# A graph-attention and a multi-head layer on one core: the order of the seven products in the projections, and when two helpers' additions may run

## The chip, the core and the metric

The kernel runs on one core of a Trainium2 chip. The metric is device time in microseconds. Before the change the median of three runs is 2658.33 us (2658.18 to 2658.8). All arithmetic is in float32. A core has a matrix engine (TensorE, in the profile PE for its products and PEld for its weight loads), a vector engine (VectorE, DVE), a scalar engine (ScalarE, ACT), GpSimd (POOL) and queues of transfers. [...]

## The reference

Input x is (64, 256, 512): 64 graphs of 256 nodes with 512 features. One adjacency matrix (256, 256) serves all. Two residual layers follow each other:

```python
# layer 0
h = jnp.maximum(_layernorm(x, axis=-1), 0.0)
x = x + _L0_gnn_ref(h, adj, L0_gnn_W, L0_gnn_a)        # one graph attention head, output [alpha@hW, hW]
# layer 1
h = jnp.maximum(_layernorm(x, axis=-1), 0.0)
x = x + _L1_gnn_ref(h, adj, Wq, bq, Wk, bk, Wv, bv, Wo, bo)

# inside layer 1, for 8 heads of 64
q = split_heads(h @ Wq.T + bq); k = split_heads(h @ Wk.T + bk); v = split_heads(h @ Wv.T + bv)
scores = jnp.einsum('bhqd,bhkd->bhqk', q, k) / 8
attn = softmax(where(adj == 0, -inf, scores))
return (attn @ v).reshape(b, n, 512) @ Wo.T + bo
```

## The kernel before

Two graphs make a group; there are 32 groups. The projections q, k and v of a group, and the output projection, are each a product of two matrices cut into quadrants, done with seven products of quadrants in place of eight (Winograd's form of Strassen's algorithm). For that, sums of the operand's quadrants are needed, made once per group by GpSimd for q, k and v, and by VectorE for the output:

```python
def not_sooner(engine, operation, *args, **kwargs):
    last = engine.last                       # the engine's last instruction so far
    after(getattr(engine, operation)(*args, **kwargs), last)

def operand_sums(engine, quads, sums):
    a11, a12, a21, a22 = quads
    not_sooner(engine, "tensor_add", sums[:, 0], a21, a22)
    engine.tensor_sub(sums[:, 1], sums[:, 0], a11)
    engine.tensor_sub(sums[:, 2], a11, a21)
    engine.tensor_sub(sums[:, 3], a12, sums[:, 1])

def seven(quads, sums):
    a11, a12, _, a22 = quads
    s1, s2, s3, s4 = (sums[:, i] for i in range(4))
    return {
        1: (a11, W11), 2: (a12, W21), 3: (s4, W22), 4: (a22, T4),
        5: (s1, T1), 6: (s2, T2), 7: (s3, T3),
    }
```

The program's scheduler is free to run an instruction of an engine ahead of one that was written earlier, if its data are there. `not_sooner` forbids that: the instruction comes after the one that was last on this engine when it was written. TensorE's whole order is fixed as written.

A projection adds the seven products up in two accumulators (PSUM banks), with copies of intermediate states kept by ScalarE and additions by VectorE:

```python
first = blocks(held_bank(turn[0], f"p{name}1_{g}"))
product(first, 1, True)
p1 = kept(first, 0, 0)                       # ScalarE: bank -> SBUF, with the bias
yield
second = blocks(mm(f"p{name}2_{g}"))
product(second, 2, True)
vector.tensor_add(part(0, 0), second, p1)
yield
product(first, 6, False)                     # onto product 1
p16 = kept(first, 0, 1)
yield
second = blocks(held_bank(1 - turn[0], f"p{name}7_{g}"))
product(second, 7, True)
p7 = kept(second, 1, 2)
yield
product(first, 5, False)
vector.tensor_add(part(1, 1), first, p7)
yield
product(second, 4, False)
vector.tensor_add(part(1, 0), second, p16)
yield
product(first, 3, False)
take(part(0, 1), first, 1)                   # ScalarE
yield
```

Each `yield` ends a piece. Pieces of different groups are interleaved by strings, one for each of the four steps of a group:

```python
steps = ("Suuunuonuonuuo", "Sssnuosuosouso", "Sususuososuos", "sSsuuousouounuonsu")
for g in range(NG):
    products = project(g + 1) ...            # "u": pieces of q, then k, then v of the next group
    pieces = first_layer(g + 2) ...          # "s": layer 0 of the group after next
    for step, parts in enumerate(steps):
        ...weigh(*waiting)                   # attention of the step before: totals, reciprocal, oT
        for part in parts: ...               # "S": scores, "o": a piece of the output projection,
                                             # "n": a piece of the next norm
        if step == 0 and g + 1 < NG:
            residual(g + 1)                  # x + b_out
```

In the first step the three "n" are: two rows' statistics, their rstd (a power on GpSimd) and normed rows xn; then their transposes xt on VectorE; then a ReLU copy hT on ScalarE. `scores` ends with two additions ps on GpSimd, after VectorE's multiplication by the mask. `residual` adds the output bias to four tiles of rows:

```python
def residual(g):
    for b in range(GB):
        for t in range(NT):
            xt = xs[g, b][:, t, :]
            gpsimd.tensor_add(xt, xt, b_out)
```

Of the kernel before, what the change touches and what calls it, by code (L numbers as in the profile page):

```python
# [57 lines left out]
def bounded(  # L58
# [24 lines left out]
    vector, scalar, gpsimd = (Remembers(e) for e in (nc.vector, nc.scalar, nc.gpsimd))  # L83
# [23 lines left out]
    def mm(name):  # L107
        return psum.tile([P, 512], F32, tag="turn", name=name, bufs=5)

    def held_bank(n, name):  # L110
        return psum.tile([P, 512], F32, tag=f"held{n}", name=name, bufs=1)

    def after(instruction, name):

        tc.add_manual_dep(
            instruction.ins, name,
            mybir.DependencyInfo(mybir.DependencyClass.NoSync, mybir.DependencyReason.DATA),
            reason="the engine's order",
        )

    def not_sooner(engine, operation, *args, **kwargs):

        last = engine.last
        after(getattr(engine, operation)(*args, **kwargs), last)
# [9 lines left out]
    def matmul(*args, **kwargs):  # L134
        in_order(nc.tensor.matmul(*args, **kwargs))  # L135
# [80 lines left out]
    b_out = const.tile([P, D], F32, name="b_out")  # L216
# [203 lines left out]

    def operand_sums(engine, quads, sums):
        a11, a12, a21, a22 = quads
        not_sooner(engine, "tensor_add", sums[:, 0], a21, a22)
        engine.tensor_sub(sums[:, 1], sums[:, 0], a11)
        engine.tensor_sub(sums[:, 2], a11, a21)
        engine.tensor_sub(sums[:, 3], a12, sums[:, 1])

    def seven(quads, sums):
# [32 lines left out]
    def first_layer(g):  # L461
# [36 lines left out]
        for r in range(GT):  # L498
# [28 lines left out]
            hT[:, 2 * c : 2 * c + 2, r * N : (r + 1) * N] for r in range(2) for c in range(2)  # L527
        ]
        operand_sums(gpsimd, quads, sums)
        operands[g] = seven(quads, sums)  # L530
        yield

    def residual(g):

        for b in range(GB):
            for t in range(NT):
                xt = xs[g, b][:, t, :]
                gpsimd.tensor_add(xt, xt, b_out)


    places = [f"place{i}" for i in range(8)]
# [1 line left out]
    def place(shape, name):  # L543
        tag = places.pop(0)
        return big.tile(shape, F32, tag=tag, name=name, bufs=1), tag
# [4 lines left out]
    def project(g):  # L550
        ops = operands.pop(g)
        for name in ("q", "k", "v"):
            shape = [P, NT, D] if name == "v" else [P, HP, N]
            dst = {}
            for b in range(GB):
                dst[b], tag = place(shape, f"{name}_{g}_{b}")
                qkv[name, g, b] = dst[b], tag
            turn[0] = 1 - turn[0]

            def blocks(bank):  # L560
                return bank.rearrange("p (o n) -> p o n", o=2)

            def product(out, i, start):
                a, w = ops[i][0], w_sb[name][:, :, ops[i][1], :]
                for o in range(2):
                    cols = slice(o * P, (o + 1) * P)
                    for c in range(2):
                        of, by = (a[:, c, cols], w[:, c, :]) if name == "v" else (w[:, c, cols], a[:, c, :])
                        matmul(
                            out[:, o, :], of, by, start=start and o == c == 0, stop=o == c == 1,  # L570
                            skip_group_check=True,
                        )

            def part(b, half):
                if name == "v":
                    return dst[b][:, :, half * D // 2 : (half + 1) * D // 2]
                return dst[b][:, 2 * half : 2 * half + 2, :]

            def take(to, bank, half):
                if name == "v":  # L580
                    scalar.copy(to, bank)
                    return
                for o in range(2):
                    i = 2 * half + o
                    scalar.activation(
                        to[:, o, :], bank[:, o, :], AF.Identity,
                        bias=bcol[name][:, i : i + 1], scale=1.0,
                    )

            def kept(bank, half, i):  # L590
                s = att.tile([P, 2, N], F32, tag="kept", name=f"kept{i}_{name}_{g}")
                take(s, bank, half)
                return s

            first = blocks(held_bank(turn[0], f"p{name}1_{g}"))
            product(first, 1, True)
            p1 = kept(first, 0, 0)
            yield
            second = blocks(mm(f"p{name}2_{g}"))
            product(second, 2, True)  # L600
            vector.tensor_add(part(0, 0), second, p1)
            yield
            product(first, 6, False)
            p16 = kept(first, 0, 1)
            yield
            second = blocks(held_bank(1 - turn[0], f"p{name}7_{g}"))
            product(second, 7, True)
            p7 = kept(second, 1, 2)
            yield
            product(first, 5, False)  # L610
            vector.tensor_add(part(1, 1), first, p7)
            yield
            product(second, 4, False)
            vector.tensor_add(part(1, 0), second, p16)
            yield
            product(first, 3, False)
            take(part(0, 1), first, 1)
            yield
# [29 lines left out]
    def weigh(g, b, quad, p, ps):  # L648


        v, v_tag = qkv["v", g, b]
        name = f"{g}_{b}_{quad}"
        total = mm(f"total_{name}")[:, :N]
        for j in range(QH):
            matmul(
                total[j * S : (j + 1) * S, :], ones[:, :S], ps[:, j, :], start=True, stop=True
            )
        r = att.tile([P, N], F32, tag="r", name=f"r_{name}", bufs=1)
        vector.reciprocal(r, total)
        pr = mm(f"pr_{name}").rearrange("p (h n) -> p h n", h=2)  # L660
        for half in range(2):
            for kb in range(NT):
                for j in range(QH):
                    c0 = (quad * QH + j) * DH + half * S
                    matmul(
                        pr[j * S : (j + 1) * S, half, :], v[:, kb, c0 : c0 + S], p[:, j, kb, :],
                        start=(kb == 0), stop=(kb == NT - 1),
                    )
        oT = big.tile([P, 2, N], F32, tag=f"oT{quad}", name=f"oT_{name}", bufs=1)
        vector.tensor_mul(oT, pr, r[:, None, :].to_broadcast([P, 2, N]))  # L670
        oTs[quad] = oT
        if quad == NQ - 1:
            places.append(v_tag)
            quads = [oTs[c][:, :, r * P : (r + 1) * P] for r in range(2) for c in range(2)]
            sums = big.tile([P, 4, 2, P], F32, tag="o_sums", name=f"o_sums_{g}_{b}", bufs=1)
            operand_sums(vector, quads, sums)
            operands["o", g, b] = seven(quads, sums)
# [51 lines left out]
    for piece, _ in enumerate(first_layer(0)):  # L729
# [7 lines left out]
        elif piece == 11:  # L737
            weight_sums("q")
    residual(0)
    products, pieces = project(0), first_layer(1) if NG > 1 else iter(())  # L740
    for i, part in enumerate("nssnsssssssssssnsn---"):
        next(products)
# [5 lines left out]
    run(verdict)  # L748


    steps = ("Suuunuonuonuuo", "Sssnuosuosouso", "Sususuososuos", "sSsuuousouounuonsu")
    waiting, late = None, iter(())
    for g in range(NG):
        products = project(g + 1) if g + 1 < NG else iter(())
        pieces = first_layer(g + 2) if g + 2 < NG else iter(())
        for step, parts in enumerate(steps):
            b, quad = divmod(step, NQ)
            if waiting is not None:
                weigh(*waiting)
                if waiting[2] == NQ - 1:  # L760
                    late = outputs(*waiting[:2])
            for part in parts:
                if part == "u":
                    next(products, None)
                elif part == "o":
                    next(late, None)
                elif part == "s":
                    next(pieces, None)
                elif part == "n":
                    next(norms, None)  # L770
                else:
                    waiting = (g, b, quad, *scores(g, b, quad))
            if step == 0 and g + 1 < NG:
                residual(g + 1)
            if step % 2 == 0 and g + 3 < NG:
                load(g + 3, b)
        run(products)
        run(pieces)
# [373 lines left out]
```

## Time and profile before

The profiled execution has a span of 2657.8 us.

| engine | busy us | share of the span |
|---|---|---|
| TensorE products (PE) | 2546.2 | 96% |
| TensorE weight loads (PEld) | 2035.1 | 77% |
| VectorE (DVE) | 1892.7 | 71% |
| GpSimd (POOL) | 993.7 | 37% |
| ScalarE (ACT) | 829.5 | 31% |

In the lines of the profile that follow, a line in the order of time begins with the start and the duration in us, then the engine, the line of the source (nearly all have the line of a helper, so the names tell them apart), the operation, output<-inputs by the program's names, the shape and the number of instructions merged in the line; in brackets the idle time of the engine before it, and what ended it. A line in the table of waits has the engine and what it was about to write, whom it waited for, and then the sum of the waits in us, their number and the longest.

The groups are alike in the middle of the run. In the stretch from 1090.5 to 1171.0 us, one group, PE was busy 78.51 of 80.50 us, DVE 58.79, POOL 30.94 and ACT 25.68.

### The profile page before, as it was taken

How to read it: one execution, taken by the hardware profiler on the slowest of the kernel's cores; microseconds unless marked ns; L12 is line 12 of the kernel's file. 1: busy time of each engine (PE TensorE's matmuls, PEld its weight loads, DVE VectorE, ACT ScalarE, POOL GpSimd, SP SyncE). 2: the span in 40 equal slices, each digit the busy share in tenths (PEclk: the TensorE clock that was granted, in tenths of full speed). 3: DMA queues.
4: the chain of work that ended last, by engine and by line, in shares of the span. 5: the costliest groups of instructions: out<-in, count | busy, mean ns of one | idle time of the engine just before them, and what ended most of it. 6: DMA issues, size and time to landing. Idle time of an engine off the chain costs nothing.

```text
span 2657.8 us, 41200 instructions
## 1 busy us (share of the span) xinstructions
PE 2546.2 (96%) x16158; PEld 2035.1 (77%) x16158; DVE 1892.7 (71%) x3103; ACT 829.5 (31%) x1759; POOL 993.7 (37%) x816
## 2 busy tenths in 40 slices
PE   6899999999999999999999999999999999999998
PEld 4677777777777777777777777877777777777776
DVE  5667678767677776687776787676777766777756
ACT  1333323333323333333233233333233333332321
POOL 3333343333343343444333434333433433433422
PEclk9999999999999999999999999999999999999999
DMA  5111222212222212222212222112222122222110
GB/s 178 48 48 64 96 80 93 83 56 72 93 83 83 82 59 80 81 95 80 72 64 88 80 96 80 64 64 96 80 88 87 57 73 88 88 80 80 47 35 33
DMA packets 129350, 205.37 MB, mean 77 GB/s; under 512 B 13952, under 2 KB 78208, under 8 KB 129152
## 3 DMA queue, kind: packets, MB, share of 16 engines
q1 hardware_dynamic: 129152, 202.69, 22.7%
q8 instruction: 129, 2.11, 0.3%
q14 instruction: 69, 0.57, 0.1%
HBM read 104.08 MB, written 98.57 MB: 76 GB/s over the span
## 4 chain that ended last, share of the span: by engine, by line
PE 53%; DVE 28%; POOL 9%; issue 7%; ACT 2%; DMA 1%; SPq 0%; DVEq 0%; ACTq 0%; POOLq 0%
PE pq L135 11%; PE py L135 10%; PE ph L135 8%; PE pv L135 7%; PE pk L135 7%; POOL sums L35 6%; PE pr L135 4%; DVE r L35 4%; PE sc L135 4%; DVE x L35 4%; DVE xn L35 3%; DVE xt L35 3%; DVE p L35 3%; POOL rstd L35 3%; DVE st L35 2%
## 5 line engine op out<-in xcount | busy, mean ns | idle before, releaser
L35 POOL TENSOR_TENSOR ps<-p 128x512 f32<-128x512 f32 x256 | 361.3, 1421 | 770.8 <-DVE p L35 770.8
L35 DVE TENSOR_TENSOR p<-p,maskT 128x1024 f32<-128x1024 f32 x256 | 434.1, 1717 | 48.3 <-ACT p L35 48.1
L35 DVE TENSOR_TENSOR x<-py,x 128x256 f32<-128x256 f32 x448 | 185.5, 414 | 350.9 <-PE py L135 343.9
L35 ACT ACTIVATE p<-sc 128x512 f32<-128x512 f32 x512 | 267.1, 602 | 382.3 <-PE sc L135 382.3
L135 PE MATMUL pq<-sums,wq_sb 128*128 128x256 f32 x1024 | 244.5, 388 | 59.2 <-POOL sums L35 59.2
L35 POOL TENSOR_TENSOR rstd<-ve,rexp 128x2 f32<-128x2 f32 x128 | 120.7, 943 | 449.9 <-DVE ve L35 444.5
L135 PE MATMUL sc<-q,k 64*128 64x256 f32 x2048 | 286.5, 393 | 0.0
L135 PEld LDWEIGHTS pq<-sums,wq_sb 128*128 128x128 f32 x1024 | 194.9, 193 | 97.6 <-POOL sums L35 71.6
L135 PEld LDWEIGHTS sc<-q,k 64*128 64x128 f32 x2048 | 203.9, 186 | 83.8 <-issue 52.6
L135 PE MATMUL py<-wo_sb,o_sums 128*128 128x256 f32 x1024 | 262.8, 380 | 2.5 <-DVE x L35 2.5
L35 DVE TENSOR_SCALAR xn<-x,mv,rstd 128x512 f32<-128x512 f32 x256 | 179.0, 730 | 109.1 <-POOL rstd L35 107.9
L135 PE MATMUL pr<-p,v 128*32 128x256 f32 x4096 | 245.5, 379 | 0.0
L135 PE MATMUL ph<-w_sb,hT 128*128 128x258 f32 x1024 | 243.6, 385 | 1.0 <-ACT hT L35 1.0
L135 PE MATMUL pv<-wv_sb,sums 128*128 128x256 f32 x1024 | 241.7, 379 | 0.0
L135 PE MATMUL pk<-sums,wk_sb 128*128 128x256 f32 x1024 | 240.2, 382 | 0.0
L35 DVE RECIPROCAL r<-total 128x256 f32<-128x256 f32 x128 | 223.3, 1744 | 16.1 <-PE total L135 16.1
L135 PEld LDWEIGHTS ph<-w_sb,hT 128*128 128x128 f32 x1024 | 192.9, 191 | 38.7 <-ACT p L35 9.9
L135 PEld LDWEIGHTS pk<-sums,wk_sb 128*128 128x128 f32 x1024 | 191.8, 190 | 35.2 <-issue 10.3
L35 POOL TENSOR_TENSOR x<-x,b_out 128x512 f32<-128x512 f32 x128 | 198.2, 1558 | 53.1 <-DVE xn L35 31.8
L135 PEld LDWEIGHTS pv<-wv_sb,sums 128*128 128x128 f32 x1024 | 194.5, 190 | 26.6 <-DVE v L35 0.3
L135 PEld LDWEIGHTS py<-wo_sb,o_sums 128*128 128x128 f32 x1024 | 192.0, 190 | 29.0 <-DVE x L35 3.3
L135 PE MATMUL py<-wo_sb,oT 128*128 128x256 f32 x768 | 200.2, 384 | 12.0 <-DVE x L35 12.0
(118 smaller groups left out, 3583.8 us busy)
## 6 DMA issues: line engine op xcount, KB each, us to landing
passed<-xt SPq DMA_DIRECT2D x124, 512.0 KB, 2.7
moved<-passed SPq DMA_DIRECT2D x496, 128.0 KB, 2.9
x<-in_x_dram SPq DMA_DIRECT2D x64, 512.0 KB, 3.9
out_dram<-x SPq DMA_DIRECT2D x64, 512.0 KB, 2.8
wq_sb<-in_L_gnn_Wq_dram SPq DMA_DIRECT2D x2, 512.0 KB, 11.9
wk_sb<-in_L_gnn_Wk_dram SPq DMA_DIRECT2D x2, 512.0 KB, 12.1
wv_sb<-in_L_gnn_Wv_dram SPq DMA_DIRECT2D x2, 512.0 KB, 11.6
wo_sb<-in_L_gnn_Wo_dram SPq DMA_DIRECT2D x8, 128.0 KB, 2.8
```

Source lines behind the costliest of these rows:

```text
L35: instruction = getattr(self.engine, operation)(*args, **kwargs)
L135: in_order(nc.tensor.matmul(*args, **kwargs))
```

## The change

The products of each projection come in the order 1, 2, 7, 6, 4, 5, 3. Product 7 needs only the difference a11 - a21, so that difference is made first, and the helper says so with `not_sooner`. The purpose is that TensorE has a product to do while GpSimd makes the sums that product 6 needs. The string of the first step is rearranged to suit. The additions of b_out, which the scheduler could run as soon as their rows were free, are held behind what GpSimd was last given to do.

```diff
     def operand_sums(engine, quads, sums):
         a11, a12, a21, a22 = quads
+        not_sooner(engine, "tensor_sub", sums[:, 2], a11, a21)
         not_sooner(engine, "tensor_add", sums[:, 0], a21, a22)
         engine.tensor_sub(sums[:, 1], sums[:, 0], a11)
-        engine.tensor_sub(sums[:, 2], a11, a21)
         engine.tensor_sub(sums[:, 3], a12, sums[:, 1])
@@ residual
-                gpsimd.tensor_add(xt, xt, b_out)
+                not_sooner(gpsimd, "tensor_add", xt, xt, b_out)
@@ project
-            product(first, 6, False)
-            p16 = kept(first, 0, 1)
-            yield
             second = blocks(held_bank(1 - turn[0], f"p{name}7_{g}"))
             product(second, 7, True)
-            p7 = kept(second, 1, 2)
+            p7 = kept(second, 1, 1)
+            yield
+            product(first, 6, False)
+            p16 = kept(first, 0, 2)
+            yield
+            product(second, 4, False)
+            vector.tensor_add(part(1, 0), second, p16)
             yield
             product(first, 5, False)
             vector.tensor_add(part(1, 1), first, p7)
-            yield
-            product(second, 4, False)
-            vector.tensor_add(part(1, 0), second, p16)
             yield
             product(first, 3, False)
             take(part(0, 1), first, 1)
@@ steps
-    steps = ("Suuunuonuonuuo", "Sssnuosuosouso", "Sususuososuos", "sSsuuousouounuonsu")
+    steps = ("Suuununuonuouo", "Sssnuosuosouso", "Sususuososuos", "sSsuuousouounuonsu")
```

## The prediction

> **What bounds the kernel now.** I read the page's shares first, then the table of waits, then the order of time on TensorE (PE), GpSimd (POOL) and VectorE (DVE) around one group's start.
>
> ```profile
> PE 2546.2 (96%) x16158; PEld 2035.1 (77%) x16158; DVE 1892.7 (71%) x3103; ACT 829.5 (31%) x1759; POOL 993.7 (37%) x816
> ```
>
> TensorE is the bound: 96% busy, one fixed instruction order, granted clock 0.994. The table of waits says what interrupts it:
>
> ```profile
> PE pq L135 <- POOL sums L35: 59.2, 31, 7.5
> PE py L135 <- DVE x L35: 14.5, 34, 1.2
> ```
>
> 31 waits of the query projection for GpSimd's sums, one at each group but the first. In order of time, around 1090 us, TensorE alone:
>
> ```profile
> 1090.62 3.72 PE L135 MATMUL pq<-hT,wq_sb 128*128 128x256 f32 x16
> 1096.02 3.72 PE L135 MATMUL pq<-sums,wq_sb 128*128 128x256 f32 x16 [1.68 <-POOL sums L35]
> ```
>
> Sixteen matmul records are products 1 and 2, so a product is 8 records; a single one started at 1100.44 and the next work at 1102.17, so a product holds TensorE 1.73 us. TensorE could have gone on at 1090.62 + 2 x 1.73 = 1094.08 and goes on at 1096.02: 1.94 us lost per group. The same three numbers return 80.5 us later, again and again: the steady period is 80.5 us. Now GpSimd and VectorE in the same stretch:
>
> ```profile
> 1090.95 2.82 POOL L35 TENSOR_TENSOR sums<-hT 128x512 f32<-128x512 f32 x2 [5.33 <-ACT hT L35]
> 1093.72 2.24 POOL L35 TENSOR_TENSOR sums<-sums,hT 128x512 f32<-128x512 f32 x1
> 1096.04 2.13 POOL L35 TENSOR_TENSOR sums<-hT,sums 128x512 f32<-128x512 f32 x1
> 1098.14 2.50 POOL L35 TENSOR_TENSOR ps<-p 128x512 f32<-128x512 f32 x2
> 1100.59 0.71 POOL L35 TENSOR_TENSOR rstd<-ve,rexp 128x2 f32<-128x2 f32 x1
> ```
> ```profile
> 1092.56 4.49 DVE L35 TENSOR_TENSOR p<-p,maskT 128x1024 f32<-128x1024 f32 x2
> ...
> 1101.34 1.00 DVE L35 TENSOR_SCALAR xn<-x,mv,rstd 128x512 f32<-128x512 f32 x2 [1.87 <-POOL rstd L35]
> 1102.26 0.41 DVE L35 TENSOR_TENSOR x<-py,x 128x256 f32<-128x256 f32 x1
> 1102.59 1.29 DVE L35 STREAM_TRANSPOSE xt<-xn 128x512 f32<-128x512 f32 x2
> 1103.81 0.65 DVE L35 TENSOR_TENSOR q<-pq,kept_q 128x512 f32<-128x512 f32 x1
> 1104.38 0.41 DVE L35 TENSOR_TENSOR x<-py,x 128x256 f32<-128x256 f32 x1
> ```
>
> GpSimd's order is sums 0 and 2 (both read hT alone), then 1, then 3. Product 6 needs sum 1, the third, which ends at 1095.96. Product 7 needs only sum 2. Second thing to see: the engines' small DVE chain xn, xt hangs on GpSimd's rstd at 1101.3, behind two ps additions, and the first query addition after it (product 5's) ends only at about 1104.5, although product 5 was done at 1102.2. TensorE's product 3 (1104.76) just escapes it.
>
> [...]p<-p,maskT takes 1209 ns at least and 2296 at most, xn 533 and 1495, GpSimd's 128x512 additions 1256 and about 2250. Instructions alternate: a VectorE operation of 1.22 us waits some 1.06 us for the GpSimd one and the reverse. Not slowed in the trace: additions that read PSUM (v<-pv,kept_v, 643 to 693 ns), statistics (633 to 696) and transposes (660 to 707). [...]product 3, accumulated into the bank of product 5, waits until VectorE has read product 5. The trace has no such wait now.
>
> **The change part by part.**
>
> (a) The order. Product 7 comes third and needs sum 2 alone, which is now made first: ready by 1092.4, long before 1094.08. Product 6 comes fourth, at 1094.08+1.73 = 1095.81, when sum 1 (1095.96, or earlier) is as good as there. Gain up to 1.73 us per group, 31 groups: 54 us, 2604 us if nothing else happened.
>
> (b) What the order costs. Between 5 and 3 stood product 4 (1.73 us) and, in the query's step, nothing else; now 3 follows 5 with only an output piece of 4 records (0.86 us) between. In the query's step VectorE must, after product 5, have added it before TensorE goes on. Work in program order ahead of that addition is now: xn twice, xt twice (the "n" of the transposes moved ahead of product 4's addition), product 4's addition, an output addition, product 5's. The program's scheduler may reorder what is ready; in the trace it kept program order at this place, and xn stood even ahead of the output addition. I take program order.
>
> (c) The quadrants' difference is also held in VectorE's own sums for the output projection (the same helper). At the group's start it was done early (o_sums<-oT, 0.42 us); it now follows oT. That puts one more VectorE operation into the alternation with GpSimd's sums. Stepping the alternation through (1.11 us held by each sum, 0.35 by o_sums, 1.2 by p) I get: sum 1 ends 1095.2, sum 3 1097.5, the two ps 1101.0 because p's second half ends 1098.6, statistics end 1101.1, rstd 1101.8: xn half a microsecond later than now.
>
> (d) The four additions of b_out per group (128 in all, 1262 ns at least, 1558 mean) run now in the value's step of the group before (1063.9 to 1077.6 in this period), as soon as their norm has read its rows. Held behind GpSimd's last operation they come after the next group's first step, the query's, and the last GpSimd operation written there is this same rstd. They are ready, so they run back to back right behind rstd[...]. A case of it is in the trace: behind an rstd at 1070.6 a ps addition started at 1072.22 and the first xn beside it took 1.41 us instead of 0.5. With four in a row both xn meet one: about 0.9+1.05 = 1.95 us more.
>
> Sum for the query's step: xn begins 1101.34 to 1101.9, its two take 1.0+1.95, xt 1.29, product 4's addition 0.65, the output's 0.41, product 5's 0.67, semaphores 0.1: product 3 can start 6.1 us after, at 1107.5 to 1108.0. Before it started at 1104.76. So not 1.7 us earlier but 2.7 to 3.3 us later, and TensorE stands idle about 4.8 us there.
>
> (e) What (d) gives back. In the value's step the moved additions slow VectorE now (a p multiply of 2.28 us at 1074.15, an xn of 1.11), which ends in the 14.5 us of py waits, 0.45 per group. These should go. But there too 3 comes one output piece after 5, and its addition is in the place of product 4's now, ending about 1084.25 where TensorE would be ready at 1083.9: 0.4 us back. Net -0.1 to -0.3.
>
> Total per group +2.5 to +3.0 us. The norm chain of the query's step runs in 30 groups; in the last projecting one there is no xn, and the gain of (a) stands: 30 x 2.75 - 2 = +80 us, 2738 us. For the case that the scheduler orders VectorE better I move the point a little: 2730.
>
> **The rivals.** First: the wait simply goes. Then 2604, or 2590 with the py waits gone as well. For it: sum 2 early enough, PE the bound; and the string of pieces was moved so that transposes come ahead, which helps if xn is early. Against it: rstd at 1101.3. Second: VectorE's order is as I say[...]: product 3 at 1105.7, +1.0 us per group, 2690. Third: the scheduler puts product 4's and the output's addition into the 1.9 us in which VectorE waits for rstd, and only xn, xt (slowed) stand before product 5's: 3 at about 1105.2 to 1105.7, or 1104 if xt is behind as well: 2640 to 2690. What speaks for order as written: xn before the output addition now, though that was ready earlier in the trace, so the scheduler believed rstd early.
>
> **Range and chances.** The main case, about 60%, gives 2711 to 2765; rivals two and three, 28%, 2635 to 2700; the first, 12%, about 2600. So 2630 to 2765 as range, chance of over 2% faster (below 2605) 0.10, within 2% 0.30, slower (above 2711) 0.60.
>
> **What would show it.** In the changed kernel the waits of pq for POOL sums should nearly vanish, 59 us to under 10; in their place pq waiting for DVE q, 30 times, some 3 to 5 us each. POOL's order: rstd, then four x<-x,b_out in a row, with xn above 1 us each beside them; p<-p,maskT's and xn's slow cases of the value's step gone; py's wait for DVE x near zero. Wrong if q's addition of product 5 runs ahead of xt, if the b_out additions do not follow rstd directly, or if the period at mid-run is below 80.5 us.

## The result and the profile after

The changed kernel takes 2748.74 us (median of four runs, 2747.06 to 2749.62) against 2658.57 of the kernel before: ratio 1.0336, 95% interval 1.0318 to 1.0354. It is slower by 3.4%, 90 us.

The shares of the page, after:

```profile
PE 2560.7 (93%) x16158; PEld 2041.3 (74%) x16158; DVE 1867.1 (68%) x3103; ACT 827.6 (30%) x1759; POOL 963.3 (35%) x816
```

TensorE has the same instructions and is busy for a smaller share: the time is in waits. The table of waits, after:

```profile
PE pq L135 <- DVE q L35: 89.1, 30, 3.0
PE pq L135 <- POOL sums L35: 45.2, 31, 2.6
...
PE pv L135 <- DVE v L35: 8.8, 30, 1.6
...
PE py L135 <- DVE x L35: 5.0, 4, 1.3
```

The wait for the sums, which the change is for, fell only from 59.2 to 45.2 us. A new one stands above it: 30 waits of the query projection for VectorE's additions q, 3.0 us each. The waits of py, the output projection, fell from 14.5 to 5.0, and a small wait came in the value projection. TensorE in order of time, one group's first step:

```profile
1127.91 1.89 PE L135 MATMUL pq<-sums,wq_sb 128*128 128x256 f32 x8
1131.22 1.99 PE L135 MATMUL pq<-sums,wq_sb 128*128 128x256 f32 x8 [1.43 <-POOL sums L35]
...
1137.37 1.03 PE L135 MATMUL py<-wo_sb,oT 128*128 128x256 f32 x4
1141.44 2.67 PE L135 MATMUL pq<-sums,wq_sb 128*128 128x256 f32 x8 [3.04 <-DVE q L35]
```

The first line is product 7, which runs without a wait; the second product 6, which waits for sum 1; the last is product 3, behind an output piece that began 4.07 us earlier and holds TensorE 0.86 us. VectorE and GpSimd there:

```profile
1125.74 4.30 DVE L35 TENSOR_TENSOR p<-p,maskT 128x1024 f32<-128x1024 f32 x2
...
1135.68 2.90 DVE L35 TENSOR_SCALAR xn<-x,mv,rstd 128x512 f32<-128x512 f32 x2 [3.13 <-POOL rstd L35]
1138.49 1.29 DVE L35 STREAM_TRANSPOSE xt<-xn 128x512 f32<-128x512 f32 x2
1139.71 0.65 DVE L35 TENSOR_TENSOR q<-pq,kept_q 128x512 f32<-128x512 f32 x1
1140.29 0.40 DVE L35 TENSOR_TENSOR x<-py,x 128x256 f32<-128x256 f32 x1
1140.62 0.67 DVE L35 TENSOR_TENSOR q<-pq,kept_q 128x512 f32<-128x512 f32 x1
```
```profile
1125.30 3.66 POOL L35 TENSOR_TENSOR sums<-hT 128x512 f32<-128x512 f32 x2 [5.95 <-ACT hT L35]
1129.04 2.13 POOL L35 TENSOR_TENSOR sums<-sums,hT 128x512 f32<-128x512 f32 x1
...
1134.93 0.71 POOL L35 TENSOR_TENSOR rstd<-ve,rexp 128x2 f32<-128x2 f32 x1
1135.61 5.31 POOL L35 TENSOR_TENSOR x<-x,b_out 128x512 f32<-128x512 f32 x4
```

The four b_out additions start the moment rstd ends, and the pair of xn beside them takes 2.90 us where it took 1.00. Behind it in VectorE's list stand xt, product 4's addition, an output addition and, last, product 5's, which ends at 1141.29; product 3 starts at 1141.44. Products 4 and 5 had been done by 1134.95 and 1137.53 (started at 1133.06 and 1135.64, 1.89 us each); their additions start at 1139.71 and 1140.62, behind xn and xt.

One more thing is in the line of product 3: it lasts 2.67 us for its 8 records, not 1.9. The granted clock of TensorE falls to one half there. In the lines of stretches that follow come the length, the busy times of PE, PEld, DVE, ACT and POOL with counts, and then PEclk as the third number from the end. The first two lines belong to this wait, which ends at 1141.44, the other two to the next group's, which ends at 1225.91 and is as long:

```profile
1139.13:1142.54 3.41, 1.10 (x5) 1.03 (x6) 2.49 (x6) 0.00 (x0) 1.79 (x2) 1.00 0.39 156
1142.54:1145.95 3.41, 3.41 (x12) 2.22 (x15) 0.10 (x1) 0.84 (x2) 0.00 (x0) 0.50 0.54 153
1221.05:1224.46 3.41, 1.82 (x9) 1.26 (x7) 3.41 (x5) 0.00 (x0) 3.41 (x4) 1.00 0.00 0
1224.46:1227.87 3.41, 1.96 (x9) 1.79 (x10) 1.63 (x4) 0.00 (x0) 0.93 (x1) 1.00 0.38 154
```

Behind the first wait the clock is 0.50 for 3.41 us, behind the second 1.00. Over the run, 4 us slices with a clock under 0.97 come at 15 places in the changed kernel, and (1 - clock) times 4 us summed over all slices from 150 to 2550 us gives 25.6 us; before it gives 1.7.

The stretches above are not cut at will. At each of the 15 places the clock is 0.50 for 3.41 us, and from the start of one to the start of the next it is 25 or 49 times 3.4133 us, to 0.02 us, so the run can be cut into windows of that length, each dip one of them. Between 150 and 2550 us TensorE is idle for 2.01 to 2.89 us in the window ahead of each dip, and for 1.97 us or less in every window that no dip follows. The first wait above lies 2.31 us within one window; the second is split by a border into 1.59 and 1.45 us.

So that kernels can be compared, I set up a ledger of one period in mid-run: from the start of one line of TensorE's order of time to the start of the next, less its records times the spacing that the same kind has when nothing waits (0.216 us for projection records, 0.1205 for scores). What is left is lost time. Gaps under 0.12 us are left out. All periods are from one start of products 1 and 2 to the next; where the clock dips, the undisturbed period is taken.

| us lost in a period | before | after |
|---|---|---|
| scores, ahead of product 1 | 0.68 | none |
| product 6 for the sums | 1.94 | 1.59 |
| product 3 of the query for VectorE | none | 3.21 |
| key's step | 0.51 | 0.51 |
| value's step: py | 0.47 | none |
| value's step: product 3, and just behind it | none | 0.61 |
| sum | 3.6 | 5.9 |
| period | 80.50 | 82.84, 84.48 with a dip |

82.84 - 80.50 = 2.34 us in 30 periods is 70 us, and the clock another 24. That is 94 against the 90 measured; the first two groups and the end of the run, in which the changed kernel is 2.0 and 2.6 us the faster, make up the rest.

### The profile page after: what moved, and what is told of

Its sections match the earlier page's. It is cut to its first block, busy times and chain, and to the rows that moved or that the text cites. A ratio compares the mean times of both kernels' runs of the same rounds, so it can differ in the third digit from the quotient of the medians.

```text
span 2747.9 us, 41075 instructions
## 1 busy us (share of the span) xinstructions
PE 2560.7 (93%) x16158; PEld 2041.3 (74%) x16158; DVE 1867.1 (68%) x3103; ACT 827.6 (30%) x1759; POOL 963.3 (35%) x816
## 4 chain that ended last, share of the span: by engine, by line
PE 75%; POOL 11%; DVE 8%; issue 3%; ACT 2%; DMA 0%; SPq 0%; ACTq 0%; DVEq 0%
PE pk L135 14%; PE pv L135 13%; PE py L135 11%; PE ph L135 8%; PE sc L135 8%; PE pr L135 8%; POOL sums L35 8%; PE po L135 4%; PE pq L135 4%; POOL ps L35 3%; PE total L135 3%; DVE xn L35 2%; DVE st L35 1%; DVE v L35 1%; DVE q L35 1%
## 5 line engine op out<-in xcount | busy, mean ns | idle before, releaser
L35 DVE TENSOR_TENSOR x<-py,x 128x256 f32<-128x256 f32 x448 | 185.2, 413 | 420.7 <-PE py L135 413.5
L35 DVE TENSOR_TENSOR p<-p,maskT 128x1024 f32<-128x1024 f32 x256 | 395.3, 1565 | 54.5 <-ACT p L35 51.0
L135 PE MATMUL pq<-sums,wq_sb 128*128 128x256 f32 x1024 | 261.7, 401 | 134.2 <-DVE q L35 89.1
L35 ACT ACTIVATE p<-sc 128x512 f32<-128x512 f32 x512 | 267.2, 601 | 395.3 <-PE sc L135 395.3
L35 DVE TENSOR_SCALAR xn<-x,mv,rstd 128x512 f32<-128x512 f32 x256 | 215.7, 873 | 154.2 <-POOL rstd L35 153.2
L135 PE MATMUL py<-wo_sb,o_sums 128*128 128x256 f32 x1024 | 275.2, 394 | 2.8 <-DVE x L35 2.6
L135 PE MATMUL sc<-q,k 64*128 64x256 f32 x2048 | 268.7, 391 | 0.0
L135 PEld LDWEIGHTS py<-wo_sb,o_sums 128*128 128x128 f32 x1024 | 201.1, 199 | 33.4 <-DVE x L35 3.4
L135 PEld LDWEIGHTS pr<-p,v 128*32 128x32 f32 x4096 | 134.3, 110 | 88.4 <-issue 1.8
```

What stands on the lines that cost most here:

```text
L35: instruction = getattr(self.engine, operation)(*args, **kwargs)
```

## The experiments

All times below are medians of four runs; the ratio is to the kernel before, measured beside them, with its 95% interval.

**The b_out additions free again.** Is it the order, the held additions, or both?

```diff
 # the changed kernel
-                not_sooner(gpsimd, "tensor_add", xt, xt, b_out)
+                gpsimd.tensor_add(xt, xt, b_out)
```

> The changed kernel with the b_out additions free again; all else as changed. Theory (VectorE's FIFO puts xn and xt ahead of product 5's addition[...]): the pair of xn falls from 2.9 to about 1.0 us, the wait of product 3 for VectorE from 3.2 to about 1.3 us per group, TensorE's clock dips (about 25 us in sum) vanish with the long waits, and about 0.45 us per group of py waits come back: 2665 to 2685 us. Rival A (the held additions cost nothing, the order alone does): stays near 2748. Rival B (only the held additions cost): 2620 or less.

2684.14 us, ratio 1.0092 (1.0076 to 1.0109). The table of waits of this kernel:

```profile
PE pq L135 <- POOL sums L35: 45.7, 32, 2.6
PE pq L135 <- DVE q L35: 34.0, 30, 1.2
```

The wait for VectorE falls from 3.2 to 1.3 us in the ledger, no slice has a low clock, the py wait of 0.48 is back, xn takes 1.00 us a pair. The order alone, without the held additions, is 0.9% slower than before; holding the additions takes the other 65 us, 24 of them through the clock.

**Only the additions held, the old product order.** The same part from the other side.

```diff
 # the kernel before
-                gpsimd.tensor_add(xt, xt, b_out)
+                not_sooner(gpsimd, "tensor_add", xt, xt, b_out)
```

> The kernel before with the b_out additions held, nothing else. Theory: they follow rstd in the query's step and slow xn by about 1.9 us; product 4 (1.73 us) still stands between 5 and 3, so product 3 starts about 1.6 us later per group, the wait for the sums stays at 1.9 us, the py waits of 0.45 us go: 2685 to 2700 us, no clock dips. Rival A (holding is free or good): 2645 to 2660.

2695.5 us, ratio 1.0135 (1.0119 to 1.0152). Its waits:

```profile
PE pq L135 <- POOL sums L35: 61.5, 31, 9.9
PE pq L135 <- DVE q L35: 45.7, 29, 1.6
```

Product 3 waits 1.74 us, although product 4 stands between 5 and 3; xn takes 2.90 us a pair here too, and the py wait is gone. The two parts of the change hurt each other: +24 and +35 us alone, +90 together. Low clock comes only with the long wait that they make up jointly: neither run alone has a 4 us slice under 0.97 between 150 and 2550 us.

**The norm put behind the additions.** If xn and xt stand in the way, let them come later.

```diff
 # the changed kernel, additions held and then free
-    steps = ("Suuununuonuouo", ...
+    steps = ("Suuuuuouonunon", ...
```

> The changed kernel with another string for the first step, in which products 4 and 5 and their additions come ahead of the norm (S, products 1 2 7 6 4, o, 5, norm, 3, o, transposes, o, copy). The additions stay held. Theory: product 5's addition no longer stands behind xn and xt, the wait for VectorE (3.2 us) and the dips go; product 6 still waits up to 1.6 us for its sum: 2620 to 2645 us. Rival C (the new product order is itself too tight, 3 right behind 5): above 2700. A risk for both: the transposes come later, and the first products of the next step may wait for them.

> As the run with the later norm, but the b_out additions free. Theory: [...]the value's step gets its py waits of 0.45 us back: 5 to 15 us slower than the held one, 2630 to 2660 us. Rival B (holding is the loss): clearly faster than the held one.

2819.88 us (1.0603, 1.0586 to 1.0621) with the additions held, 2721.4 (1.0232, 1.0215 to 1.0249) with them free. Both expectations were far off, and the free additions, expected to be 5 to 15 us slower than the held ones, are 98 us faster. Product 3's wait did go (0.2 us in the ledger). It reappeared further down the same list; TensorE of the held one:

```profile
1091.99 2.07 PE L135 MATMUL sc<-q,k 64*128 64x256 f32 x6 [2.63 <-DVE r L35]
1094.00 6.06 PE L135 MATMUL ph<-w_sb,hT 128*128 128x258 f32 x16
```

The next step's scores wait for the reciprocal r (which frees the bank of the totals), and r now stands behind xn and xt: 2.98 us lost, then a clock dip that costs 3.7 us in this group, where it lasts two windows (56.4 us over the run), then 0.81 us more for hT, as the transposes started later. With free additions the same two losses are 1.07 and 0.81. The risk was named for hT, not for r. What it shows: in the query's step VectorE has no slack to hide xn and xt in; there the question is only which instruction of TensorE is made to wait for them.

**The scores behind products 1 and 2.** Those two need only the ReLU output of the first graph, and TensorE can do them and the scores while GpSimd makes the sums. VectorE's mask multiplications, which belong to the scores, then come after the sums. Product 5 and its output piece also go ahead of the transposes.

```diff
 # the kernel before, its product order, nothing held
-    steps = ("Suuunuonuonuuo", ...
+    steps = ("uuSunuouonnuuo", ...
```

> The kernel before (products 1 2 6 7 5 4 3, nothing held) with another string for the first step: products 1 and 2 run ahead of the scores, product 5 and its output piece ahead of the transposes. Theory: GpSimd makes its four sums while TensorE does 1, 2 and the scores, and VectorE's mask multiplications come after the sums instead of alternating with them; product 6's wait of 1.9 us goes, and product 5's addition stands ahead of xt, so no new wait of more than 0.3 us comes: 2595 to 2620 us. Rival D (VectorE's work in the query's step is the bound whatever the order): the wait only moves, above 2645.

2587.92 us, ratio 0.9737 (0.972 to 0.9753): 2.6% faster than the kernel before. GpSimd in this kernel, in order of time:

```profile
1062.59 2.49 POOL L35 TENSOR_TENSOR sums<-hT 128x512 f32<-128x512 f32 x2 [1.92 <-ACT hT L35]
1065.03 1.28 POOL L35 TENSOR_TENSOR sums<-sums,hT 128x512 f32<-128x512 f32 x1
1066.39 1.33 POOL L35 TENSOR_TENSOR sums<-hT,sums 128x512 f32<-128x512 f32 x1
1070.36 3.42 POOL L35 TENSOR_TENSOR ps<-p 128x512 f32<-128x512 f32 x2 [2.64 <-DVE p L35]
```

Sum 1 takes 1.28 us in place of 2.24 and is there at 1066.31; TensorE wants it at 1068.64. The period is 78.08 us, 1.16 of it lost. The expectation had been 7 us too careful: of the scores' 0.68 us too only 0.19 is left. The two moves of the string, the scores and product 5, were not tried apart in this order of products.

The same with the changed kernel's order, to see what product 6 still waits for:

```diff
 # the changed kernel, additions free
-    steps = ("Suuununuonuouo", ...
+    steps = ("uuSununuonuouo", ...
```

> The changed kernel with free b_out additions (2684 us) and the scores behind products 1 and 2. Theory: the 1.5 us that product 6 still waits are the mask multiplications [...], so they go; but xn and xt still stand ahead of product 5's addition, so about 0.6 to 1 us of it comes back as product 3's wait (1.2 us now): 2640 to 2665 us. If the sums are slow for another reason, product 6 still waits over 1 us.

2639.29 us, ratio 0.993 (0.9913 to 0.9946). Product 6 no longer waits at all (1.57 before this edit), and product 3 waits 1.21 us, against 1.32 before the edit: rstd ends 11.6 us after the first instruction behind the attention's products in place of 13.3, so it came earlier by as much as TensorE did. Of the 0.6 to 1 us that I expected to come back there, nothing did.

**More work in the wait.** Is the clock low because TensorE was idle?

```diff
 # the changed kernel
+            if name == "q":
+                product(blocks(mm(f"fill_{g}")), 1, True)
             product(first, 3, False)
```

> The changed kernel with one more product of the query (product 1 once more, into a bank that nothing reads), 1.73 us of TensorE's time put right ahead of product 3. Theory (the clock dips come from TensorE's long idle, and the filler lies in time that is idle anyway): the wait falls from 3.2 to 1.5 us, the dips vanish, 2715 to 2730 us, faster with more work. Rival E (the dips have another cause, or are an effect of the records): 2745 to 2752. Rival F (the wait is not for VectorE, the filler adds its time): 2795 or more.

2724.44 us, ratio 1.0249 (1.0232 to 1.0266): 24 us faster than the changed kernel, with 32 more products. TensorE in order of time:

```profile
1129.86 1.89 PE L135 MATMUL fill<-hT,wq_sb 128*128 128x256 f32 x8
1133.06 1.97 PE L135 MATMUL pq<-sums,wq_sb 128*128 128x256 f32 x8 [1.31 <-DVE q L35]
```

The wait is 1.47 us in the ledger, the period 82.84, exactly the undisturbed one of the changed kernel, and no slice has a low clock.

**Product 7 ahead of 6, and no more.**

```diff
 # the changed kernel, additions free, string of before; products 1 2 7 6 5 4 3
-            product(second, 4, False)
-            vector.tensor_add(part(1, 0), second, p16)
-            yield
             product(first, 5, False)
             vector.tensor_add(part(1, 1), first, p7)
             yield
+            product(second, 4, False)
+            vector.tensor_add(part(1, 0), second, p16)
+            yield
```

> The changed kernel with products 4 and 5 back in the order of before (1 2 7 6 5 4 3), the string of before and free b_out additions: of the change only 7 ahead of 6 and the difference made first. Theory: product 3 no longer waits for VectorE beyond 0.4 us, product 6 still waits about 1.5 us as the mask multiplications alternate with the sums, product 5 may wait 0.3 us for the kept copy of product 6: 2645 to 2660 us. Rival G (7 ahead of 6 alone brings its full 1.7 us): 2600 to 2615.

2687.45 us, ratio 1.0112 (1.0095 to 1.0129), 27 us above the top of what I expected. Its waits:

```profile
PE pq L135 <- DVE q L35: 31.3, 29, 1.1
PE pk L135 <- ACT kept_k L35: 28.8, 31, 0.9
...
PE pq L135 <- POOL sums L35: 10.7, 31, 4.7
```

Here product 6 loses 0.32 us only: 7 ahead of 6 can bring nearly its full 1.7 us, against what I expected of this run. But it is lost again at once: product 3 waits 1.23 us for VectorE, which did not come earlier, and in the key's step product 5 follows 6 onto the same bank with nothing between and waits for ScalarE's copy of it (1.19 us lost). I had seen that hazard for the query (0.24 measured) and overlooked the key. It is what product 4 between 6 and 5 is good for in the change.

**The difference not made first.**

```diff
 # the changed kernel
-        not_sooner(engine, "tensor_sub", sums[:, 2], a11, a21)
         not_sooner(engine, "tensor_add", sums[:, 0], a21, a22)
         engine.tensor_sub(sums[:, 1], sums[:, 0], a11)
+        engine.tensor_sub(sums[:, 2], a11, a21)
```

> The changed kernel with the quadrants' difference back in its old place in the helper, all else as changed. Theory: GpSimd's list has it second in any case, product 7 needs it 3.5 us after the sums begin and it is there after 2.8, so nothing: 2740 to 2755 us. Rival (product 7 needs it first): product 7 waits, over 2765.

2743.12 us, ratio 1.0315 (1.0297 to 1.0332), which overlaps the changed kernel's interval. The reason given was wrong, though the time was right: product 7 does wait, 0.98 us, as the two sums ahead take 3.55 us, more than the 2.8 of before; product 6 then waits 0.48 in place of 1.59. The same delay in another place. Its clock dips, behind the same wait for product 3, sum to 22.2 us.

**The additions held elsewhere.** Is it that they are held, or where?

```diff
-            if step == 0 and g + 1 < NG:
+            if step == 1 and g + 1 < NG:
                 residual(g + 1)
```

once in the changed kernel, once in the one with the scores behind products 1 and 2 (there with `not_sooner` as in the change):

> The changed kernel with the b_out additions held but written one step later, nothing else. Theory: xn falls back to 1.0 us a pair, product 3 waits 1.3 us in place of 3.2, no clock dips, and no py wait in the value's step either: 2660 to 2675 us, below the 2684 of the free additions. Rival (holding costs wherever it is): near 2748.

> The kernel with the scores behind products 1 and 2 (2588 us), and the b_out additions held, but written one step later, so that they follow the key step's H additions, where VectorE has 7 of 20 us of work. Theory (what counts is where they meet VectorE, not that they are held): the py wait of 0.47 us in the value's step goes, no other comes: 2568 to 2580 us. Rival (that py wait is not theirs): 2585 to 2590.

2708.02 us (1.0187, 1.017 to 1.0204) and 2610.72 us (0.9821, 0.9804 to 0.9837). In the first, xn, the clock and the py wait behave as expected, but both times lie above the range that I expected, by 33 and 31 us: the additions now meet the attention exponents of layer 0 at the end of the key's step. VectorE of the second:

```profile
1108.86 2.78 DVE L35 SCALAR_TENSOR_TENSOR e<-e 128x512 f32<-128x512 f32 x2
1111.56 1.75 DVE L35 RECIPROCAL r<-total 128x256 f32<-128x256 f32 x1
```

The pair e<-e takes 1.37 us when nothing meets it; r comes 1.4 us later and the scores lose 1.45 us in place of 0.38. The last run puts them behind the first H addition of the same step instead (GpSimd's x<-H,x, which adds a part of layer 0's result to its rows), where VectorE is done with its mask multiplications and has not begun with e:

```diff
 # the kernel of the run with 2587.92 us, additions held
-            for part in parts:
+            for i, part in enumerate(parts):
+                if step == 1 and i == 2 and g + 1 < NG:
+                    residual(g + 1)
                 ...
-            if step == 0 and g + 1 < NG:
-                residual(g + 1)
```

> The kernel with the scores behind products 1 and 2 (2588 us), the b_out additions held behind the first H addition of the key step: after that step's two mask multiplications and before its attention exponents' multiplication by the mask on VectorE. Theory (what counts is which VectorE operations they meet): neither the py wait of the value's step (0.47 us) nor the wait of the scores for the reciprocal that the later place brought (1.45 us in place of 0.38): 2568 to 2580 us. Rival (holding costs wherever it is put): 2588 or more.

2568.48 us, ratio 0.9662 (0.9646 to 0.9678): 3.4% faster than the kernel before. The shares of its page:

```profile
PE 2513.7 (98%) x16158; PEld 2033.3 (79%) x16158; DVE 1825.0 (71%) x3103; ACT 830.2 (32%) x1759; POOL 922.3 (36%) x816
```

VectorE and GpSimd, with the same instructions, are busy 67.7 and 71.4 us less than before: by that much these instructions are shorter in sum. The four b_out additions, for one, take 4.95 us together in mid-run, where one took 1.56 us on average before. Additions that read PSUM hardly differ between the kernel before and the changed one: those of q took 64.8 and 63.9 us in sum, k 64.9 and 64.9, v 64.4 and 64.5, the output's 185.5 and 185.2, while the mask multiplications took 434.1 and 395.3 and xn 179.0 and 215.7. The period is 77.50 us, 0.71 lost.

## Why the prediction was right

The time predicted was 2730 us, in a range of 2630 to 2765; measured 2748.74. The main case held in its mechanism; four of its steps had the wrong size, and one cause was missing.

- **(a), product 7 needs only the difference and runs at once: right. Product 6 then finding sum 1 as good as there: wrong** (1.59 us lost, not some 0.1, and the waits for the sums fell to 45.2 us, not under 10). Step (c) had sum 1 at 1095.2, 7.2 us after the scores' start (1088.01); it came at 1131.17, 8.8 after it (1122.36). I had let the alternation begin with VectorE's small o_sums. These were done by 1125.63, as VectorE was ahead of TensorE by then, and both long mask multiplications came ahead of sum 1's end: they took 2.09 and 2.29 us (1.21 at least in this trace) and ended at 1127.83 and 1130.04, between the ends of sums 2, 0 and 1 at 1126.76, 1128.96 and 1131.17. The times of the sums show it: from the start of the first to the end of sum 1 they take 5.87 us in the changed kernel. In the run with 7 ahead of 6 alone the last of the o_sums still meets a sum (1.38 us in place of 0.42); there the sums take 5.12, and product 6 loses 0.32 us. In the run of the changed order with the scores behind products 1 and 2, where the multiplications come after the sums, they take 3.91, and the 1.96 us saved are more than the whole wait; that the sums start earlier there, and that TensorE has the scores to do, adds to it. How far VectorE is ahead depends on the order of products and not on the b_out additions: in mid-run the rstd of the value's step ends 0.72 us ahead of the next attention totals in the changed order, whether the additions are held, free or later, and 0.1 us in the order of before, whether they are free or held. The changed order makes TensorE lose 0.61 us for product 3 just ahead of that point; that this is the reason is only argued.
- **(b), VectorE's order xn, xt, product 4's addition, the output's, product 5's: right**, instruction by instruction. What stood between products 5 and 3 before was misread: in the query's step there was an output piece besides product 4, 2.59 us in all. Nothing in the sum rests on it, as that sum sets out from product 3 at 1104.76.
- **(c), xn half a microsecond later: wrong.** rstd ends 13.3 us after the scores' start, before and after. With (a) it moves nothing in the end, since product 3's start hangs on rstd and on what VectorE does behind it; the loss merely divides into 1.59 and 3.21 us instead of 0 and 4.8.
- **(d), the b_out additions right behind rstd, xn 1.95 us slower: right.** Measured 1.90, and both runs that change only the holding confirm it, one in each order of products. The sum from the scores' start to product 3 was predicted to grow by 2.7 to 3.3 us; it grew from 16.75 to 19.08, 2.33: the half microsecond of (c) is not there, and from xn's start to product 3 it is 5.76 us, not 6.1.
- **(e), the py waits gone and 0.4 us back in the value's step: right in kind** (0.47 gone; 0.41 and another 0.20 behind it came), but the net is 0.14 us lost, where 0.1 to 0.3 gained was predicted. Not seen: the scores' 0.68 us ahead of product 1, which is gone after the change.
- **Missing: the clock.** 24 of the 90 us are TensorE at a lower clock, 0.50 for 3.41 us behind a long wait, and the sum had nothing for it. In the changed kernel a dip follows each window with 2.01 us of idle time or more, and none with 1.97 or less. Dips come behind waits in which TensorE is idle for 3.04 us (the changed kernel, 15 of 28 waits in mid-run), for 2.63 us (the late norm with held additions, 27 of 28) and for 3.02 us (one wait near the end of the kernel before), and in mid-run in none of the ten kernels sliced in this way whose waits are 1.7 us at most. In the changed kernel they sum to 25.6 us, 1.7 each. The filler shows the cause: with its waits of 1.47 us no dip is left. By chance the misses nearly cancel: the sum per group, 2.5 to 3.0 predicted, was 2.34 in waits and 0.8 in clock.

The lines of the kernel before that (b) misread, the output piece behind product 5, product 4 and product 3:

```profile
1102.17 1.03 PE L135 MATMUL py<-wo_sb,oT 128*128 128x256 f32 x4
1103.03 1.89 PE L135 MATMUL pq<-hT,wq_sb 128*128 128x256 f32 x8
1104.76 1.89 PE L135 MATMUL pq<-sums,wq_sb 128*128 128x256 f32 x8
```

Of the rivals, the second (xn not slowed by the b_out additions, 2690) is what the kernel comes to in time with free additions, 2684, though with its loss divided between products 6 and 3. The first, that the wait simply goes, does not hold for this order of products in any run; it is nearest in the run with 7 ahead of 6 alone, and there too the gain is lost in two other waits. The third, additions moved up into VectorE's wait for rstd, did not happen: VectorE stands idle there for 3.13 us, and xn comes first.

## What to carry to other kernels

A wait of the bounding engine is best followed one engine further before work is moved into it: here TensorE waited for GpSimd's sums, but the next thing due, product 3, hung on VectorE's list, and on a GpSimd result in it, so with that result no earlier the reordering could only change which product waits. Work "held back" on GpSimd still has to be put somewhere, and where it lengthens VectorE's instructions (the pair of xn 2.90 us beside the b_out additions, 1.00 without), the place is to be chosen by what VectorE does there: holding the same four additions cost 65 us behind rstd in the changed kernel, and gave 19 us behind an H addition in the kernel with the scores behind products 1 and 2. A string of pieces that puts independent products and the scores ahead of the sums' use did what the change was meant for.

## What the runs showed of the hardware that I had not expected

A TensorE that is idle for 3 us may pay again afterwards, and whether it does depends on where the idle time lies: in the changed kernel half clock for a window of 3.41 us followed when 2.01 us or more of the window before were idle, which was so for 15 of 28 waits of 3.04 us. 32 useless products of 1.73 us, put into these waits, made the kernel 24 us faster. And where VectorE's and GpSimd's instructions run beside each other, both sides can get longer: in the kernel before a mask multiplication took 2.28 us in place of 1.21 and sum 1 beside it 2.24, against 1.28 in the run where the multiplications come after the sums. So the difference between two kernels with the same instructions can be read from busy time: from the kernel before to the last run VectorE's and GpSimd's busy sums fell by 68 and 71 us.
